# A graph layer ahead of three attention layers: block loop in four parts, one step of the open groups per part, row candidates taken one block later

## Chip, cores and metric

The kernel runs on one core of a Trainium2 chip. The metric is the device time of one launch in microseconds: the median of the timed runs is 3094.89 us (3094.21 to 3097.0, three runs). One further execution was recorded by the profiler; it took 2503.29 us.

## What is computed

The inputs are 3327 nodes with 256 features, `x`, and an adjacency matrix `adj` of 3327 x 3327 integers, 0 or 1, with about 16 ones in a row. Four layers follow one another. Cut to what matters here:

```
# layer 0
h = x @ Wt.T + bt                                  # 64 wide
s = leaky_relu(h @ Wa.T + ba, 0.2)                 # one number per row
w = softmax(where(adj > 0, s, -9e15), axis=1)
y = x + (w @ h) @ Wp.T + bp
x = gamma * (y - mean(y)) * rsqrt(var(y) + 1e-5) + beta
# layers 1, 2, 3
q, k, v = split(layer_norm(x) @ w_qkv)             # 8 heads of 32
attn = softmax(where(adj != 0, q @ k.T * scale, -inf))
x = x + (attn @ v) @ w_proj + b_proj
x = x + gelu(layer_norm(x) @ w1 + b1) @ w2 + b2
```

In layer 0 a row has one score for all its neighbours, so its softmax needs only the sum of `h` over the neighbours, the sum over all nodes and the number of neighbours.

## The kernel before

**Stages.** The rows form 26 blocks of 128. First `x` is loaded, `h` is computed and split into three bf16 parts beside a column of ones (`hs`). Then comes the block loop of layer 0 (L576 to L620), which reads the adjacency matrix once and makes two things of it: the neighbour sums and each row's list of neighbours. Then `order()` sorts the rows by their number of neighbours, and the three attention layers follow, which gather the keys and values of the listed neighbours one by one. Only the block loop and what runs in it is changed.

**One block.** `load(i)` brings 128 rows of `adj` (1.66 MB) into one of three int32 buffers by a DMA that SP issues; `cast(i)` turns them into bf16 on ACT (L269), into one of three buffers `abf`, whose pad columns POOL clears (L266). PE transposes the block in 26 pieces of 128 x 128, eight to a PSUM tile (L586; two such tiles, `pt`), and ACT copies each tile to `aT` by a sign function (L587). In the next iteration PE multiplies `aT` by `hs` in 26 matmuls (L590), and ACT copies the sum to `acc` (L600). For the lists DVE multiplies the block in place by the column numbers (L614, `num`) and takes the eight largest of each of 13 stretches of 256 columns (L617); these 104 candidates and the number of neighbours go to DRAM (L603, L604).

**Order in an iteration before.** The instructions are emitted in the order of the code and no scheduler moves them, so each engine works through its own queue in that order. Iteration `i` emits four times "eight transposes of block i, their sign copy, eight matmuls of block i-1" (the fourth time two of each); then the `acc` copy of block i-1 and its candidate DMAs; `cast(i+2)` and `load(i+4)`; one round of the open groups; the multiplication and the 13 maxima of block i; and a second round.

**Open groups and rounds.** When the last block of a group (`FIN`, mostly four blocks; the last groups have three, two and one) has its sums, `finish(f)` is opened for it. It is a generator: `steps(1)` is one round, in which each open group emits its next piece, up to its next `yield`. The pieces of a group of four, with the letters that the text uses:

- a (L404 to L437): counts and two score weights on DVE, their exponentials on ACT (L425, L426), prefix counts on PE, `seen` on POOL
- b (L439 to L453): the weighted neighbour sums `hn` on DVE
- c (L455 to L459): transposes of `hn` on PE, copy `nT` on ACT
- d (L461 to L471): product with `Wp` on PE (L466), addition to `x` on DVE (L470), addition of `bp` on POOL (L471)
- e (L473, L474): the rows' mean and variance on DVE (L126, L127), a power of -1/2 on POOL (L130)
- f (L476 to L484): one factor on DVE (L477), normalization on ACT (L479), gain and shift on POOL (L483, L484)
- g (L486): empty
- h (L487 to L489): the same moments for layer 1, and the rows to DRAM
- then for each of two pairs of blocks: i, normalization (DVE L137, then ACT L141); j, transposes on PE (L151) and their copy on ACT (L153); k and l, the q, k and v rows of one block each (PE L171 and L176, ACT L173 and L178) with their DMAs (L502, L503)

So a group of four has 16 pieces, and two rounds per iteration take it through eight iterations: in the steady part two groups are open at a time.

Of the kernel before, what the change touches and what calls it, by code (L numbers as in the profile page):

```python
# [8 lines left out]
FP = mybir.dt.float32  # L9
# [9 lines left out]
P = 128  # L19
# [12 lines left out]
NB = (N + P - 1) // P  # L32
# [28 lines left out]
def kernel(ctx: ExitStack, tc: tile.TileContext, ins, out: bass.AP):  # L61
# [136 lines left out]
    def node_list(b):  # L198

        t = nodes_[b]  # L200
        cd = t[:, 2 * D:2 * D + CAND]
        nr = (CAPS[b] + 7) // 8
        w = 8 * nr

        cg = lists.tile([P, CAND], FP, tag="cg", bufs=2, name=f"cg_{b}")
        nc.vector.scalar_tensor_tensor(cg, cd, 0.0, segb.rearrange("p s k -> p (s k)"), ALU.is_gt, ALU.mult)
        nc.vector.tensor_add(cg, cg, cd)
        ls = lists.tile([P, LW], FP, tag="ls", bufs=2, name=f"ls_{b}")
        for k in range(nr):
            nc.vector.max(out=ls[:, 8 * k:8 * k + 8], in_=cg)  # L210
            if k < nr - 1:
                nc.vector.match_replace(out=cg, in_to_replace=ls[:, 8 * k:8 * k + 8], in_values=cg, imm_value=0.0)
        em = lists.tile([P, LW], FP, tag="em", bufs=2, name=f"em_{b}")
        own = lists.tile([P, 1], FP, tag="own", bufs=2, name=f"own_{b}")
        nc.vector.tensor_scalar(em[:, :w], ls[:, :w], 0.5, None, ALU.is_lt)
        nc.vector.tensor_scalar(own, pf[:, b:b + 1], 1.0, None, ALU.add)
        nc.vector.scalar_tensor_tensor(ls[:, :w], em[:, :w], own, ls[:, :w], ALU.mult, ALU.add)
        nc.vector.tensor_scalar(idx[:, b, :w], ls[:, :w], -1.0, None, ALU.add)
        nc.vector.tensor_scalar(bias[:, b, :w], em[:, :w], NEG, None, ALU.mult)
        nc.vector.tensor_reduce(found[:, b, 0:1], em[:, :w], AX.X, ALU.add)  # L220
        nc.scalar.copy(found[:, b, 1:2], t[:, 2 * D + CAND:])


    with ExitStack() as st, tc.manual_schedule():
# [145 lines left out]
                h_rows(m - 1)  # L370
        cast(0)
        h_rows(len(PAIRS) - 1)
        cast(1)
        load(3)

        allb = [P, NB, H0]
        nc.vector.tensor_mul(rest, h_sb, wa_b[:, None, :].to_broadcast(allb))
# [14 lines left out]
        def finish(f):  # L392
# [62 lines left out]
            pt = big(f"ptn_{f}")  # L455
            for j in range(n):
                nc.tensor.transpose(pt[:H0, j * P:(j + 1) * P], hn[:, j, :], ident)
            nT = l0w.tile([H0, 4 * P], FP, tag="nT", bufs=1, name=f"nT_{f}")
            nc.scalar.copy(nT[:, :n * P], pt[:H0, :n * P])  # L459
            yield  # L460
            pps = []  # L461
            for j0 in range(0, n, 2):
                m = min(2, n - j0)
                ps = big(f"pp_{f}_{j0}").rearrange("p (b d) -> p b d", d=D)
                for j in range(j0, j0 + m):
                    nc.tensor.matmul(ps[:, j - j0, :], nT[:, j * P:(j + 1) * P], wpT, start=True, stop=True)  # L466
                pps.append((j0, m, ps))
            for j0, m, ps in pps:
                xi = x0[:, b0 + j0:b0 + j0 + m, :]
                nc.vector.tensor_add(xi, xi, ps[:, :m, :])  # L470
# [9 lines left out]
            for j0 in range(0, n, 2):  # L480
# [1 line left out]
                xi = x0[:, b0 + j0:b0 + j0 + m, :]  # L482
                nc.gpsimd.tensor_tensor(xi, xi, gam_b[:, None, :].to_broadcast([P, m, D]), ALU.mult)  # L483
                nc.gpsimd.tensor_add(xi, xi, bet_b[:, None, :].to_broadcast([P, m, D]))  # L484
            yield
            yield  # L486
            mv, rs = moments(views, f"q1_{f}")  # L487
            for i in blocks:
# [82 lines left out]
        def gains_in():  # L571
            pt = big("pt_cols")
            nc.tensor.transpose(pt[:, :P], cols, ident)
            nc.vector.tensor_copy(pv, pt[:, :48].rearrange("p (l k) -> p l k", l=3))

        for i in range(NB + 1):  # L576
            if i < NB:
                aTs[i] = l0w.tile([P, NB, P], BF, tag="aT", bufs=3, name=f"aT_{i}")
            if i:
                pa = ps_a.tile([P, 512], FP, tag="acc", name=f"pa_{i - 1}")  # L580
            for k0 in range(0, NB, 8):
                kn = min(8, NB - k0)
                if i < NB:
                    pt = ps_t.tile([P, 8, P], BF, tag="pt", name=f"pt_{i}_{k0}")
                    for m in range(kn):
                        nc.tensor.transpose(pt[:, m, :], abfs[i][:, (k0 + m) * P:(k0 + m + 1) * P], ident_bf)  # L586
                    nc.scalar.activation(aTs[i][:, k0:k0 + kn, :], pt[:, :kn, :], AF.Sign)  # L587
                if i:
                    for k in range(k0, k0 + kn):
                        nc.tensor.matmul(pa[:, :3 * H0 + 1], aTs[i - 1][:, k, :], hs[:, k, :],  # L590
                                         start=(k == 0), stop=(k == NB - 1))
            if i == 0:
                gains_in()
            if i == 1:
                bias_rows()
            if i:
                f, j = in_fin[i - 1]
                if j == 0:
                    accs[f] = l0w.tile([P, 4, 3 * H0 + 1], FP, tag="acc", name=f"acc_{f}")
                nc.scalar.copy(accs[f][:, j, :], pa[:, :3 * H0 + 1])  # L600
                cand = cands.pop(i - 1)
                nc.scalar.copy(cand[:, CAND:], accs[f][:, j, 3 * H0:])
                nc.sync.dma_start(cand_dr[(i - 1) * P:i * P, :], cand)  # L603
                nc.sync.dma_start(node_dr[(i - 1) * P:i * P, 2 * D:], cand)  # L604
            if i + 2 < NB:
                cast(i + 2)
                if i + 4 < NB:
                    load(i + 4)
            if i == NB:
                break  # L610
            steps(1)

            ab3 = abfs.pop(i).rearrange("p (s c) -> p s c", s=SEGS)
            nc.vector.tensor_mul(ab3, ab3, num)  # L614
            cands[i] = cand = l0w.tile([P, CAND + 1], FP, tag="cand", name=f"cand_{i}")
            for m in range(SEGS):
                nc.vector.max(out=cand[:, 8 * m:8 * m + 8], in_=ab3[:, m, :])  # L617
            if i and i - 1 in last_of:
                under.append(finish(last_of[i - 1]))
            steps(2 if i >= NB - 3 else 1)  # L620
        under.append(finish(last_of[NB - 1]))
        steps(1)
        under.append(order())
        while under:
# [465 lines left out]
```

## Time and profile before

| what | value |
|---|---|
| median of the timed runs | 3094.89 us |
| the profiled execution | 2503.29 us |
| its span, first to last instruction | 2501.5 us |
| its mean granted TensorE clock | 0.798 |
| busy in the span: PE, DVE, ACT, POOL | 1674.9, 1788.8, 794.1, 1485.3 us |
| start to the block loop | 0 to 42 us |
| block loop, to the last `acc` copy | 42 to 363.4 us |
| rest of layer 0 and of the sort, to the first gather of the layers | 363.4 to 414.3 us |
| attention layers | 414.3 to 2501.5 us |
| starts of the `acc` copies of blocks 0, 3, 7, 11, 15, 19, 25 | 51.8, 72.3, 110.8, 169.0, 223.7, 278.4, 363.4 us |

Times in the profile are microseconds from the span's start. In a view of waits a line names the instruction that waited, who ended the wait, then the total in us, the number of times and the longest. In a timeline a line has the start, the duration, the engine, the line of code, the operation with its output and inputs, and in brackets the idle time of the engine just before, with what ended it. In a table of windows each line has a stretch, its length, the busy time of PE, PE's weight loads, DVE, ACT and POOL with instruction counts, the granted clock, the share of the DMA engines and GB/s.

### The profile page before, as it was taken

What the parts mean: (1) busy time and instruction counts of PE and PEld (TensorE: products, weight loads), DVE (VectorE), ACT (ScalarE), POOL (GpSimd) and SP (SyncE); (2) the same over time, 40 slices, a digit from 0 to 9 for tenths busy, and PEclk for the clock granted to TensorE, in tenths of its full rate; (3) what the DMA queues carried; (4) which work ended last, traced back from release to release, by engine and by line L of the source; (5) the groups of instructions that cost most, each with busy time, mean ns of one, the idle gap of its engine ahead of it and who ended that gap; (6) DMA issues with size and microseconds to landing.
All of it is one profiled execution on the core that took longest, in us unless ns stands there. A gap on an engine that the chain in (4) does not pass through costs nothing. (4 is left out here: it accounts for less than half of the span.)

```text
span 2501.5 us, 25704 instructions
## 1 busy us (share of the span) xinstructions
PE 1674.9 (67%) x8346; PEld 1313.9 (53%) x8346; DVE 1788.8 (72%) x3214; ACT 794.1 (32%) x1464; POOL 1485.3 (59%) x1666
## 2 busy tenths in 40 slices
PE   7567663476678766683678787776837766766567
PEld 6445542355556545562566566554625655545455
DVE  6975684977789888743876787777437777777772
ACT  5766652132232222231143232222311323111222
POOL 1222235766667777615767677776157777777761
PEclk9788876588878887796778888878967888877777
DMA  6655515766567777616766677776167666666660
GB/s 238 210 169 167 158 60 173 210 197 176 165 188 215 209 211 208 182 49 212 205 186 200 189 213 217 212 210 187 46 198 207 194 200 192 201 204 190 198 181 11
DMA packets 158408, 452.79 MB, mean 181 GB/s; under 512 B 34367, under 2 KB 61641, under 8 KB 154937
## 3 DMA queue, kind: packets, MB, share of 16 engines
q0 software_dynamic: 111264, 363.68, 49.9%
q1 hardware_dynamic: 46636, 87.24, 10.6%
q8 instruction: 69, 1.13, 0.2%
q14 instruction: 75, 0.61, 0.1%
q10 hardware_dynamic: 364, 0.13, 0.0%
HBM read 410.64 MB, written 40.28 MB: 180 GB/s over the span
## 5 line engine op out<-in xcount | busy, mean ns | idle before, releaser
L758 POOL DMA_INDIRECT sl<-kv,idx x1290 | 1229.5, 953 | 400.1 <-issue 334.1
L805 PE MATMUL po<-ident,sl 128*128 128x128 f32 x2580 | 473.3, 347 | 601.5 <-DVE sl L802 600.7
L805 PEld LDWEIGHTS po<-ident,sl 128*128 128x128 f32 x2580 | 394.6, 180 | 673.6 <-DVE sl L802 665.1
L769 DVE TENSOR_TENSOR sl<-sl,qp 128x1024 f32<-128x1024 f32 (+1 forms) x354 | 397.1, 1122 | 239.5 <-DMA sl<-kv,idx 202.1
L770 DVE TENSOR_REDUCE sc<-sl 128x32 f32<-128x1024 f32 (+1 forms) x354 | 398.3, 1125 | 12.0
L802 DVE TENSOR_TENSOR sl<-sl,qp 128x1024 f32<-128x1024 f32 (+1 forms) x354 | 389.1, 1119 | 2.6
L685 PE MATMUL pu<-fT,w 128*128 128x256 f32 (+1 forms) x1344 | 329.3, 394 | 36.0 <-ACT fT L153 36.0
L698 PE MATMUL pd<-w,gT 128*128 128x256 f32 x1248 | 314.7, 407 | 28.4 <-ACT gT L689 28.4
L685 PEld LDWEIGHTS pu<-fT,w 128*128 128x128 f32 x1344 | 256.5, 207 | 77.4 <-ACT fT L153 44.7
L698 PEld LDWEIGHTS pd<-w,gT 128*128 128x128 f32 x1248 | 249.7, 206 | 76.1 <-ACT gT L689 32.6
L689 ACT ACTIVATE gT<-pu,pv 128x256 f32<-128x256 f32 (+1 forms) x336 | 134.9, 456 | 264.5 <-PE pu L685 260.4
L171 PE MATMUL pk<-wq,hT 128*128 128x512 f32 x312 | 177.9, 699 | 32.7 <-ACT hT L153 32.7
L141 ACT ACTIVATE xn_f<-x_sb,nmu_f,rsig_f 128x256 f32<-128x256 f32 x78 | 42.8, 593 | 366.3 <-DVE nmu_f L137 352.4
L703 DVE TENSOR_TENSOR x_sb<-x_sb,pd 128x512 f32<-128x512 f32 (+1 forms) x42 | 27.2, 648 | 166.0 <-PE pd L698 166.0
L811 ACT COPY oT<-po 128x256 f32<-128x256 f32 x78 | 29.0, 372 | 367.8 <-PE po L805 367.5
L666 DVE TENSOR_TENSOR x_sb<-x_sb,pp 128x512 f32<-128x512 f32 (+1 forms) x42 | 27.3, 649 | 133.3 <-PE pp L664 133.1
L617 DVE MAX8 cand<-abf 128x8 f32<-128x256 bf16 x338 | 113.0, 410 | 1.7
L171 PEld LDWEIGHTS pk<-wq,hT 128*128 128x128 f32 x312 | 63.2, 223 | 86.2 <-issue 40.6
L720 POOL DMA_INDIRECT kv<-kvr,perm x52 | 52.5, 1011 | 90.4 <-ACT kvr L173 76.9
L586 PE MATMUL pt<-ident_bf,abf 128*128 128x128 bf16 x676 | 59.9, 232 | 49.9 <-ACT aT L587 49.8
L664 PE MATMUL pp<-w_proj,oT 128*128 128x256 f32 x312 | 91.3, 441 | 1.1 <-issue 0.2
L176 PEld LDWEIGHTS pq<-wq,hT 128*128 128x128 f32 x312 | 64.3, 206 | 49.8 <-issue 39.3
(220 smaller groups left out, 2018.3 us busy)
## 6 DMA issues: line engine op xcount, KB each, us to landing
a<-in_adj_dram SPq DMA_DIRECT2D x25, 1663.5 KB
sl<-kv,idx POOLq DMA_INDIRECT x1290, 3.7
kv<-kvr SPq DMA_DIRECT2D x26, 256.0 KB
q<-qr SPq DMA_DIRECT2D x52, 128.0 KB
q<-q SPq DMA_DIRECT2D x52, 128.0 KB
w<-in_L_gnn_w_dram SPq DMA_DIRECT2D x6, 1024.0 KB
node<-x SPq DMA_DIRECT2D x26, 128.0 KB
node<-qr SPq DMA_DIRECT2D x26, 128.0 KB
```

What stands on the lines that cost most here:

```text
L171: nc.tensor.matmul(pk, hT[:, c, :], wq[:, c, D:], start=(c == 0), stop=(c == 1))
L176: nc.tensor.matmul(pq[:, :D], hT[:, c, :], wq[:, c, :D], start=(c == 0), stop=(c == 1))
L617: nc.vector.max(out=cand[:, 8 * m:8 * m + 8], in_=ab3[:, m, :])
L664: nc.tensor.matmul(pp[:, j, :], oT[:, c, j * P:(j + 1) * P], w["w_proj"][:, c, :], start=False, stop=(c == 1 and j == n - 1))
L685: nc.tensor.matmul(pu[:, a, :n * P], w["w1"][:, c, f * P:(f + 1) * P], fT[:, c, :n * P], start=(c == 0), stop=(c == 1))
L689: nc.scalar.activation(gT[:, f0 + a, :n * P], pu[:, a, :n * P], AF.Gelu_apprx_tanh, bias=pv[:, L - 1, 8 + f:9 + f])
L698: nc.tensor.matmul(pd[:, j, :], gT[:, f, j * P:(j + 1) * P], w["w2"][:, h * FH + f, :], start=False, stop=(h == 1 and f == FH - 1 and j == ...
L758: nc.gpsimd.indirect_dma_start(out=t[:, k - a, :], out_offset=None, in_=kv_dr[self.L][:, :], in_offset=bass.IndirectOffsetOnAxis(ap=idx[:, ...
L769: nc.vector.tensor_mul(kq, kq, self.qp[:, None, :D].to_broadcast([P, n, D]))
L770: nc.vector.tensor_reduce(self.sc[:, a:z, :], kq.rearrange("p s (h d) -> p s h d", h=HEADS), AX.X, ALU.add)
L802: nc.vector.tensor_mul(vv, vv, self.pw[:, a:z, :, None].to_broadcast([P, n, HEADS, HD]))
L805: nc.tensor.matmul(self.po[:, c, :], t[:, k, D + c * P:D + (c + 1) * P], ident, is_transpose=True, start=False, stop=(a + k == self.S - 1 ...
```

## The change

The iteration is cut into four parts, one for each PSUM tile of transposes. A part emits the transposes and the sign copy of block i; in the second part also `cast(i+1)` and `load(i+3)`; then the matmuls of block i-1; then a share of the candidate work of block i-1 instead of block i (the multiplication and 2 of the 13 maxima in the first part, then 4, 4 and 3); and one round of the open groups. The candidate work thus stands one block behind the transposes, and there are four rounds in each iteration instead of two, from the first iteration on; a new group opens at an iteration's end and has its first round in the next iteration. In `finish` piece c is cut in two (c1 the transposes, c2 the copy), d in two (d1 the product, d2 the additions), and the empty piece g is taken out: 17 pieces. `cast(0)` and `cast(1)` still stand ahead of the loop, `load(3)` now between them; a small tile of the list building, `own`, has one buffer instead of two.

```diff
@@ node_list
-        own = lists.tile([P, 1], FP, tag="own", bufs=2, name=f"own_{b}")
+        own = lists.tile([P, 1], FP, tag="own", bufs=1, name=f"own_{b}")
@@ ahead of the loop
+        load(3)
         cast(1)
-        load(3)
@@ finish
                 nc.tensor.transpose(pt[:H0, j * P:(j + 1) * P], hn[:, j, :], ident)
+            yield
             nT = l0w.tile([H0, 4 * P], FP, tag="nT", bufs=1, name=f"nT_{f}")
...
                 pps.append((j0, m, ps))
+            yield
             for j0, m, ps in pps:
                 xi = x0[:, b0 + j0:b0 + j0 + m, :]
                 nc.vector.tensor_add(xi, xi, ps[:, :m, :])
...
                 nc.gpsimd.tensor_add(xi, xi, bet_b[:, None, :].to_broadcast([P, m, D]))
-            yield
             yield
             mv, rs = moments(views, f"q1_{f}")
@@ the block loop
             if i:
                 pa = ps_a.tile([P, 512], FP, tag="acc", name=f"pa_{i - 1}")
-            for k0 in range(0, NB, 8):
+                ab3 = abfs.pop(i - 1).rearrange("p (s c) -> p s c", s=SEGS)
+                cand = l0w.tile([P, CAND + 1], FP, tag="cand", name=f"cand_{i - 1}")
+            for part, k0 in enumerate(range(0, NB, 8)):
...
                     nc.scalar.activation(aTs[i][:, k0:k0 + kn, :], pt[:, :kn, :], AF.Sign)
+                if part == 1:
+                    if 0 < i < NB - 1:
+                        cast(i + 1)
+                    if i + 3 < NB and i:
+                        load(i + 3)
+                    if i == 0:
+                        gains_in()
+                    if i == 1:
+                        bias_rows()
                 if i:
                     for k in range(k0, k0 + kn):
                         nc.tensor.matmul(pa[:, :3 * H0 + 1], aTs[i - 1][:, k, :], hs[:, k, :],
                                          start=(k == 0), stop=(k == NB - 1))
-            if i == 0:
-                gains_in()
-            if i == 1:
-                bias_rows()
+
+                    if part == 0:
+                        nc.vector.tensor_mul(ab3, ab3, num)
+                    for m in range(*((0, 2), (2, 6), (6, 10), (10, SEGS))[part]):
+                        nc.vector.max(out=cand[:, 8 * m:8 * m + 8], in_=ab3[:, m, :])
+                steps(1)
             if i:
...
                 nc.scalar.copy(accs[f][:, j, :], pa[:, :3 * H0 + 1])
-                cand = cands.pop(i - 1)
                 nc.scalar.copy(cand[:, CAND:], accs[f][:, j, 3 * H0:])
                 nc.sync.dma_start(cand_dr[(i - 1) * P:i * P, :], cand)
                 nc.sync.dma_start(node_dr[(i - 1) * P:i * P, 2 * D:], cand)
-            if i + 2 < NB:
-                cast(i + 2)
-                if i + 4 < NB:
-                    load(i + 4)
-            if i == NB:
-                break
-            steps(1)
-
-            ab3 = abfs.pop(i).rearrange("p (s c) -> p s c", s=SEGS)
-            nc.vector.tensor_mul(ab3, ab3, num)
-            cands[i] = cand = l0w.tile([P, CAND + 1], FP, tag="cand", name=f"cand_{i}")
-            for m in range(SEGS):
-                nc.vector.max(out=cand[:, 8 * m:8 * m + 8], in_=ab3[:, m, :])
-            if i and i - 1 in last_of:
-                under.append(finish(last_of[i - 1]))
-            steps(2 if i >= NB - 3 else 1)
-        under.append(finish(last_of[NB - 1]))
+                if i - 1 in last_of:
+                    under.append(finish(last_of[i - 1]))
         steps(1)
         under.append(order())
```

## The prediction

> **What bounds the kernel now.** I read the table of windows first, for the steady part: the four blocks from the `acc` copy at 169.0 to the one at 223.7 us, and the stretch after the loop.
>
> ```profile
> 169.00:223.70 54.70, 36.48 (x275) 27.85 (x274) 37.23 (x108) 36.42 (x52) 12.78 (x17) 0.81 0.53 172
> 363.40:414.30 50.90, 32.19 (x117) 17.61 (x116) 30.88 (x118) 17.22 (x42) 16.48 (x68) 0.83 0.35 111
> ```
>
> Four blocks take 54.7 us, PE, DVE and ACT are each busy for about 37, DMA for half. No engine is the bound: the loop is bound by waits among three in-order queues. The next four blocks (223.7 to 278.4) take the same 54.7. So I read the waits of the block loop (42 to 366 us), and then the timeline about the longest of them.
>
> ```profile
> PE pt L586 <- ACT aT L587: 49.8, 17, 7.2
> ACT xn_q L141 <- DVE nmu_q L137: 45.0, 10, 7.6
> DVE x L470 <- PE pp L466: 42.5, 10, 10.4
> ACT kvr L173 <- PE pk L171: 25.8, 11, 5.0
> ```
>
> ```profile
> 198.30 4.14 POOL L471 TENSOR_TENSOR x<-x,rowb 128x512 f32<-128x512 f32 x2 [10.61 <-DVE x L470]
> ...
> 201.41 4.35 DVE L617 MAX8 cand<-abf 128x8 f32<-128x256 bf16 x13
> 205.67 0.14 DVE L137 SCALAR_TENSOR_TENSOR nmu_q<-mv_q,rsig_q 128x2 f32<-128x2 f32 x1
> 205.85 1.09 ACT L141 ACTIVATE xn_q<-x,nmu_q,rsig_q 128x256 f32<-128x256 f32 x2 [7.59 <-DVE nmu_q L137]
> 207.90 1.01 PE L586 MATMUL pt<-ident_bf,abf 128*128 128x128 bf16 x8 [7.17 <-ACT aT L587]
> ```
>
> Piece i's 0.14 us factor stands on DVE behind the multiplication and 13 maxima; ACT waits 7.59 us for it with the next sign copies behind it, and so PE waits 7.17. That costs once per four blocks.
>
> ```profile
> 160.12 2.07 ACT L479 ACTIVATE x<-x,nm,rsig_l 128x256 f32<-128x256 f32 x4
> 161.35 1.27 POOL L483 TENSOR_TENSOR x<-x,rowb 128x512 f32<-128x512 f32 x1 [6.92 <-ACT x L479]
> ...
> 164.00 0.43 DVE L126 BATCH_NORM_STATS2 st_q<-x 128x6 f32<-128x256 f32 x1 [2.03 <-POOL x L484]
> ...
> 166.58 0.43 DVE L126 BATCH_NORM_STATS2 st_q<-x 128x6 f32<-128x256 f32 x1 [1.41 <-POOL abf L266]
> ```
>
> The chain e to h is visible here: ACT, four POOL operations of 1.27, then moments that DVE can begin only pair by pair. Even with the empty piece g between, DVE waits 2.03 and 1.41.
>
> **What the skill says.** (1) The Trainium skill, "TensorE: Matmul & The Clock Gate", section "Architectural detail": ACT and DVE are strict FIFO, only PE pulls weight loads forward. The 7.59 us wait agrees. (2) Same page, "What's actually happening": an idle PE drops to half clock and returns after sustained work. The trace agrees: after 7.17 idle, eight transposes take 1.01 instead of 0.61; a PE wait of 3.75 before 185.2 is followed by an L171 of 3.61 instead of 1.91. (3) "SBUF — State Buffer", section "Who interferes with whom": a DVE operation with two SBUF inputs contends with POOL's reads, one with a single input doesn't. Agrees: L614 takes 2.32 beside L471, 1.89 elsewhere.
>
> **The change, laid out by hand.** I put the four queues side by side with these durations: eight transposes and eight matmuls 1.13 from start to start; sign copy 0.9, the last 0.4; cast 2.96; `acc` and `cand` copies 0.5 together; multiplication 1.9, maxima 0.335 each, so DVE shares of 2.6, 1.4, 1.4 and 1.1. Pieces: a 3.2 on DVE, its exponentials ready 2.4 in; b 3.3; product of d 2.0 on PE, additions 1.4; e 2.2, then 1.3 to the power; f 2.07 on ACT, then POOL about 5.1; h ends 1.2 after POOL, the power 1.1 more; i 1.1, j 0.5 on PE and 1.0 on ACT; k or l 2.7 on PE at full clock (5.1 at half), copies 0.95. ACT's own work per block is 6.6 (the copies at 66.0 and 72.3 are 6.3 apart, without a group).
>
> A group now takes 17 rounds, so mostly one is open. The four iterations, ended by `acc` and `cand` copies, follow ACT:
> - A (l of the old group with a; b; c1; c2): ACT busy 8.9. It waits 1.6: for L171 and L176 in the first part and for the transposes behind them. 10.5 us.
> - B (d1; d2; e; f): busy 8.7. The second transposes stand behind the 2.0 us product: 1.4. The additions end 5 us into the iteration, POOL needs 2.6, the moments and the power follow; ACT reaches f with its four sign copies done and waits 2.8. 12.9 us.
> - C (h; i; j; k): busy 9.7. POOL ends gain and shift 3.5 into the iteration, the power comes 3 later, and ACT at i waits 1.9; then 2.1 for k's matmuls. 13.7 us.
> - D (l; i; j; k): busy 10.6, two waits of 1.4 and 2.1 for L171 and L176. 13.9 us.
>
> Sum 51.0 at full clock. PE now idles 4.7 and 5.0 in C and 3.4 in D; idles of that length are followed by half clock in the trace. Two of the four k/l then cost 2.4 more, two j 0.4 more: 56.6. I take 56, for 54.7 now.
>
> What goes: ACT's 9.4 for L137 and DVE's 10.2 for L466 (the two waits of the 54.7). The DVE wait costs nothing in itself: its cover is ACT's 37 busy us and its waits. What is late next is the chain d2 to i: its five rounds used to lie 6 us apart with a block of DVE work between them; now 2 to 3. Removing g brings h one round nearer to POOL's four operations.
>
> Moved beside other work, at nothing: the candidates one block behind take away L614's wait for transposes (2.2 per cycle, DVE only). L617 ends one iteration later; the candidate DMAs on SP wait for it and `load` stands behind them, but it is issued two iterations, over 12 us, ahead of its cast, as before, and DMA is busy for 0.53. If that cover fails, a load's 7 us (1.66 MB at 240 GB/s) comes on the path. `load(3)` still waits for `cast(0)`. L266 stands on POOL behind h's power; the instruction order of the changed program lists the cast of iteration C as waiting for its DMA alone, so only the next block's last transposes need L266. The wait on `own` is among DVE's own operations. `finish`'s DMAs keep their order among themselves; k's rows are issued once per part rather than twice in a row.
>
> Block by block: to the copy at 72.3 no group is open, ACT bounds at 6.3 per block: 0. Blocks 4 to 7: before 38.5, since the first group gets two rounds per iteration and is alone; now a whole cycle without l, A 12.8 as its DVE lead is missing, 53.3 plus 1 to 5 for clock: +18. Blocks 8 to 11: before 58.2, now 56: -2. Blocks 12 to 19: 2 x 1.5 = +3. Blocks 20 to 25: before 85.0; now 10.5 + 12.9 + 13.7, then 16 (D with a to c of the group of three), 15, and 14 for the last without sign or cast, 82.1, plus 5.6: +3. After the loop: before 7, 10 and 11 pieces are left of the last three groups, now 4, 9 and 12. The last takes 44 us from 365.5 for its 11, 4 each: +4 for one more, -4 for fewer companions (-6 to +5): 0. Sum +22; with full clock throughout +15 - 7 - 7 - 3 = -2. I take +15, nearer the throttled end.
>
> On the profiled execution: 2503.3 + 15 = 2518. The timed median is 591.6 us above it; the profile doesn't show where, so I carry the difference over unchanged: 3094.9 + 15 = 3110. If it scaled with the time it would be +19, inside the range.
>
> **Rivals.**
> - Faster: the chain e to i is hidden. Place: ACT at f and i. The waits of 2.8 and 1.9 vanish if the parts of B and C last 3.9 us or more on the other engines, and if the closer spacing keeps PE at full clock. The cycle is 51.0 - 4.7 = 46.3: four later cycles give 4 x -8.4 = -34, the first +10: -24, 3071; if k/l are covered too, another 4 x 3.5 less: 3057. For it: ACT is busy only 37 of 54.7. Against: each piece still needs the one before from another engine, one short part earlier.
> - No change: full clock, chain as laid out: -2, 3093.
> - Worse: POOL contention (L471 took 4.14 for two, where I took 2.6) and half clock in all four k/l instead of two. Place: iterations B, C and D; it decides once the multiplication of the next part meets L471, or PE idles over 3.4 us in A too. 1.5 + 4.8 = 6.3 per cycle, over the four later cycles +25 on top of the +15: 3135; half of it, 3122. For it: both have been seen in this trace. Against: L471 now stands beside maxima, which read one operand.
> - The change doesn't do what it says: would the rounds be taken unevenly, two groups would stay open. The code forbids it: one call per part.
>
> **Chances.** Forecast, with its own range 3102 to 3120, 0.41; worse 0.14; no change 0.12; faster 0.33. Within 0.2% means 3088.7 to 3101.1, about what a measurement of this kernel can tell from no change. Faster 0.33, same 0.12, slower 0.55. The range reaches from the faster rival's second figure to the worse one's end: 3057 to 3135.
>
> **What would show it.** Right: cycles of four blocks of 54 to 58 us between `acc` copies; no wait of ACT for L137 above 3; new waits of ACT for L477 and of DVE for L484; L171 of 3.6 in iteration C. The step for the first group is right if block 7's copy comes at about 128 instead of 110.8. It is wrong if ACT's waits for L477 and L137 together are under 2 us per four blocks, or if the cycle is under 50. The layers' part should keep its 2087 us.

## The result, and the profile after

| | before | after |
|---|---|---|
| median of 12 timed runs each | 3094.55 us (3086.81 to 3104.66) | 3092.6 us (3075.4 to 3098.8) |
| ratio, 95% interval | | 0.9984 (0.9966 to 1.0003) |
| profiled execution | 2503.29 us | 3086.38 us |
| starts of the `acc` copies 3, 7, 11, 15, 19, 25 | 72.3, 110.8, 169.0, 223.7, 278.4, 363.4 | 74.8, 127.6, 178.7, 229.9, 281.1, 365.1 |
| first gather of the layers (L187) | 414.3 us | 412.4 us |

The change made no difference that these runs can tell: -2 us, where +15 was forecast. The attention layers of every kernel here take some 590 us more in most sets of runs than in one (the kernel before has a median of 2503.6 us in one set below and 3091 to 3115 in the rest), so ratios are formed within a set only, and what the change does is read from the stage ahead of the layers, which repeats within 5 us (first gather at 414.3 and 418.9 before, 412.4 and 411.0 after).

The lines of the changed kernel shift: transposes L586 are now L591, sign copy L592, matmuls L604, multiplication L608, maxima L610, `acc` copy L616; L466, L470, L471 are L467, L472, L473; L477, L479 are L479, L481; L483, L484 are L485, L486.

The table of windows of the changed kernel, for a steady cycle of four blocks and for the stretch from the last `acc` copy to the first gather (columns as before):

```profile
178.70:229.90 51.20, 35.91 (x278) 26.62 (x276) 36.51 (x107) 35.97 (x53) 11.48 (x16) 0.83 0.56 183
365.06:412.40 47.34, 26.39 (x86) 13.58 (x84) 29.90 (x106) 12.44 (x32) 15.54 (x68) 0.71 0.28 90
```

The busy times are those of before (36, 37, 36); the cycle went from 54.7 to 51.2, so 3.5 us of waiting went. The cycles from block 8 to block 19 all take 51.1 or 51.2. Which waits are left, from the view of waits in that cycle:

```profile
DVE abf L608 <- PE pt L591: 8.4, 1, 8.4
PE pn_q L151 <- ACT xn_q L141: 8.2, 2, 5.5
ACT kvr L173 <- PE pk L171: 7.2, 4, 2.7
...
PE pt L591 <- ACT aT L592: 4.9, 3, 2.8
...
DVE st_q L126 <- POOL x L486: 3.1, 2, 1.7
ACT xn_q L141 <- DVE nmu_q L137: 2.4, 1, 2.4
ACT x L481 <- DVE nm L479: 2.2, 1, 2.2
```

The two long waits of before (ACT for L137 in one piece of 7.6, DVE for L466 of 10.1) are gone. In their place stand many waits of 1.5 to 8 us, most of them of an engine for the one group's next link. (The 8.4 of L608 is another kind: DVE has run out of candidates and of the group's work in iteration D, and stands ahead of the next multiplication until the block's last transposes are made.) The timeline of iteration C shows a stretch of that chain:

```profile
201.99 1.27 POOL L486 TENSOR_TENSOR x<-x,rowb 128x512 f32<-128x512 f32 x1
203.29 0.43 DVE L126 BATCH_NORM_STATS2 st_q<-x 128x6 f32<-128x256 f32 x1 [1.67 <-POOL x L486]
...
205.87 0.43 DVE L126 BATCH_NORM_STATS2 st_q<-x 128x6 f32<-128x256 f32 x1 [1.40 <-POOL x L486]
...
207.32 1.02 POOL L130 TENSOR_TENSOR rsig_q<-rsig_q,mhalf 128x4 f32<-128x4 f32 x1 [1.49 <-DVE rsig_q L129]
...
208.64 1.09 ACT L141 ACTIVATE xn_q<-x,nmu_q,rsig_q 128x256 f32<-128x256 f32 x2 [2.44 <-DVE nmu_q L137]
209.30 1.18 PE L151 MATMUL pn_q<-ident,xn_q 128*128 128x128 f32 x4 [5.52 <-ACT xn_q L141]
...
211.15 3.38 PE L171 MATMUL pk<-wq,hT 128*128 128x512 f32 x4
...
214.36 1.03 PE L176 MATMUL pq<-wq,hT 128*128 128x256 f32 x4
214.56 0.59 ACT L173 COPY kvr<-pk 128x512 f32<-128x512 f32 x1 [2.73 <-PE pk L171]
```

POOL, DVE, POOL, ACT, PE, ACT: from 202.0 to 214.6 each line with a bracket starts when the one named there ends. PE waits 5.52 and its next products take 3.38 in place of 1.91. It is not the only stretch of slow rows in a cycle; these are the rows of d's product and of iteration D:

```profile
189.12 1.99 PE L467 MATMUL pp<-wpT,nT 64*128 64x256 f32 x8
...
224.03 1.18 PE L151 MATMUL pn_q<-ident,xn_q 128*128 128x128 f32 x4 [2.65 <-ACT xn_q L141]
...
225.89 2.83 PE L171 MATMUL pk<-wq,hT 128*128 128x512 f32 x4
```

As to the layers, their table of windows before and after (the first is of the kernel before):

```profile
420.00:2501.50 2081.50, 1401.44 (x6323) 1101.87 (x6323) 1492.70 (x2340) 546.25 (x1106) 1379.60 (x1460) 0.79 0.63 184
```

```profile
420.00:3084.50 2664.50, 1525.93 (x6323) 1167.23 (x6323) 1487.57 (x2340) 542.34 (x1105) 1381.37 (x1458) 0.72 0.49 144
```

Instruction counts agree to 2, and the busy times of DVE, ACT and POOL to 5 us; PE is busy 125 us longer. Most of the 583 us are waits. The longest of a new kind have no releaser in this program (the profile calls it "remote"), in the waits of the changed kernel's layers:

```profile
ACT gT L689 <- remote: 328.3, 20, 27.4
...
ACT oT L811 <- remote: 204.5, 9, 41.6
```

Since the timed runs of both kernels hold it, it is no part of the change.

### The profile page after: what moved, and what is told of

Same layout as the page of the kernel before. It is cut to its first block, busy times and chain, and to the rows that moved or that the text cites. A ratio compares the mean times of both kernels' runs of the same rounds, so it can differ in the third digit from the quotient of the medians.

```text
span 3084.5 us, 25707 instructions
## 1 busy us (share of the span) xinstructions
PE 1806.9 (59%) x8346; PEld 1380.3 (45%) x8346; DVE 1775.9 (58%) x3214; ACT 790.0 (26%) x1464; POOL 1479.2 (48%) x1666
## 4 chain that ended last, share of the span: by engine, by line
PE 25%; another core or an unknown queue 19%; issue 16%; DVE 13%; POOL 7%; ACT 5%; DMA 2%; SPq 0%; DVEq 0%; POOLq 0%; ACTq 0%
PE pd L698 7%; POOL sl L758 6%; PE po L805 5%; PE pu L685 4%; PE pk L171 4%; DVE sl L769 3%; DVE sl L802 3%; PE pp L664 2%; DVE sc L770 2%; PE pq L176 2%; DMA sl<-kv,idx 1%; ACT gT L689 1%; DMA q<-q 1%; ACT L689 1%
## 5 line engine op out<-in xcount | busy, mean ns | idle before, releaser
L805 PE MATMUL po<-ident,sl 128*128 128x128 f32 x2580 | 493.6, 354 | 690.0 <-DVE sl L802 521.4
L805 PEld LDWEIGHTS po<-ident,sl 128*128 128x128 f32 x2580 | 410.0, 185 | 764.6 <-DVE sl L802 558.2
L698 PE MATMUL pd<-w,gT 128*128 128x256 f32 x1248 | 355.8, 445 | 224.5 <-ACT gT L689 194.5
L685 PE MATMUL pu<-fT,w 128*128 128x256 f32 (+1 forms) x1344 | 356.7, 411 | 99.0 <-issue 50.7
L698 PEld LDWEIGHTS pd<-w,gT 128*128 128x128 f32 x1248 | 274.6, 227 | 293.3 <-ACT gT L689 208.1
L685 PEld LDWEIGHTS pu<-fT,w 128*128 128x128 f32 x1344 | 267.7, 216 | 151.7 <-issue 61.7
L689 ACT ACTIVATE gT<-pu,pv 128x256 f32<-128x256 f32 (+1 forms) x336 | 134.9, 458 | 542.9 <-remote 328.3
L171 PE MATMUL pk<-wq,hT 128*128 128x512 f32 x312 | 199.8, 775 | 89.2 <-ACT hT L153 78.0
L130 POOL TENSOR_TENSOR rsig_f<-rsig_f,mhalf 128x2 f32<-128x2 f32 (+1 forms) x42 | 29.2, 696 | 292.3 <-DVE rsig_f L129 273.7
L720 POOL DMA_INDIRECT kv<-kvr,perm x52 | 52.6, 1012 | 225.0 <-ACT kvr L173 161.0
L811 ACT COPY oT<-po 128x256 f32<-128x256 f32 x78 | 29.1, 374 | 475.0 <-remote 204.5
L171 PEld LDWEIGHTS pk<-wq,hT 128*128 128x128 f32 x312 | 70.6, 248 | 155.5 <-ACT hT L153 88.8
L610 DVE MAX8 cand<-abf 128x8 f32<-128x256 bf16 x338 | 116.5, 411 | 1.9
L130 POOL TENSOR_TENSOR rsig_h<-rsig_h,mhalf 128x2 f32<-128x2 f32 (+1 forms) x28 | 19.5, 695 | 196.2 <-DVE rsig_h L129 196.2
```

Of the source, the lines that this page charges most:

```text
L171: nc.tensor.matmul(pk, hT[:, c, :], wq[:, c, D:], start=(c == 0), stop=(c == 1))
L685: nc.tensor.matmul(pu[:, a, :n * P], w["w1"][:, c, f * P:(f + 1) * P], fT[:, c, :n * P], start=(c == 0), stop=(c == 1))
L689: nc.scalar.activation(gT[:, f0 + a, :n * P], pu[:, a, :n * P], AF.Gelu_apprx_tanh, bias=pv[:, L - 1, 8 + f:9 + f])
L698: nc.tensor.matmul(pd[:, j, :], gT[:, f, j * P:(j + 1) * P], w["w2"][:, h * FH + f, :], start=False, stop=(h == 1 and f == FH - 1 and j == ...
L805: nc.tensor.matmul(self.po[:, c, :], t[:, k, D + c * P:D + (c + 1) * P], ident, is_transpose=True, start=False, stop=(a + k == self.S - 1 ...
```

## The experiments

The edits of e7 and e11 are shown against the kernel before, that of e8 against e2, that of e10 against e4, all others against the changed kernel. Theory 1: the cycle is the latency of the chain of pieces of the one open group. Theory 2: PE's idle times and the half clock after them are the cost. Theory 3: what counts is the place of the candidates. "Cycle" is half the time between the `acc` copies of blocks 11 and 19, two cycles of four blocks. "Loop" is the time from the `acc` copy of block 3 to the first gather, which leaves out how early the first loads came (the copy of block 3 lies between 68 and 75 us in all profiles). Ratios are to the kernel before in the same set.

| kernel | steps per block, groups open | candidates | blocks 4-7 | cycle | loop | ratio (95%) |
|---|---|---|---|---|---|---|
| before | 2, two | own block | 38.5 | 54.7 | 342.0 | 1 |
| before, again | 2, two | own block | 41.4 | 54.6 | 344.0 | |
| after | 4, one | behind, spread | 52.8 | 51.2 | 337.6 | 0.9984 (0.9966 to 1.0003) |
| after, again | 4, one | behind, spread | 52.0 | 51.2 | 336.9 | 0.9984 (0.997 to 0.9997) |
| e1 copies a step later | 4, one | behind, spread | 48.9 | 54.6 | 349.5 | 1.0031 (1.0015 to 1.0046) |
| e2 two steps | 2, two | behind, spread | 35.8 | 43.5 | 305.6 | 0.9855 (0.9835 to 0.9876) |
| e3 PE kept busy | 4, one | behind, spread | 50.8 | 49.8 | 333.7 | 0.997 (0.9955 to 0.9984) |
| e4 own block | 4, one | own block | 60.2 | 61.6 | 387.6 | 1.0216 (1.0188 to 1.0244) |
| e7 behind alone | 2 at the end, two | behind, one stretch | 36.4 | 52.3 | 336.9 | 0.9982 (0.9969 to 0.9994) |
| e8 one stretch | 2, two | behind, one stretch | 38.2 | 48.0 | 326.4 | 0.9949 (0.992 to 0.9978) |
| e9 alternate | 4 stops, two | behind, spread | 36.2 | 43.1 | 309.9 | 0.9886 (0.9857 to 0.9915) |
| e10 parts only | 2, two | own block | 41.5 | 46.1 | 320.1 | 0.9905 (0.9874 to 0.9935) |
| e11 one step moved | 2, two | own block | 41.1 | 47.7 | 315.8 | 0.9906 (0.9881 to 0.9932) |
| e12 steps in pairs | 4, one | behind, spread | 51.5 | 52.8 | 340.8 | 0.9975 (0.9961 to 0.9988) |
| e13 groups drained | all at once | behind, spread | 73.9 | 73.2 | 485.2 | 1.0508 (1.0473 to 1.0542) |

**The kernel before again.**

> The kernel before, run once more, because its profiled execution lasted 2503 us where all its timed runs lasted about 3095. Every theory expects the stage before the layers to be the same as in the profile shown (first gather of a layer, L187, at 414 us, within 1 us). If the 590 us were a property of that one execution, this profile has a layers' part of about 2665 us, like that of the changed kernel.

Its first gather came at 418.9, 4.5 us later and not within the 1 us expected; 2.5 of that is there at the copy of block 3 already, so the loop repeats within 2 us. The layers' part did not turn out 2665: 2090.8 us from the first gather, in a set in which all 20 timed runs of the kernel before lay between 2499 and 2512. So 2503 is not the accident of one execution: it is a level that holds for a whole set of runs.

**e1, copies of k and l a step later.**

```diff
-                    kv, q = qkv_rows(l0w, big, wq1, hT[...], 1, f"1_{i}")
+                    pk, pq = qkv_products(big, wq1, hT[...], f"1_{i}")
+                    yield
+                    kv = ...; nc.scalar.copy(kv, pk)
+                    q = ...; nc.scalar.copy(q, pq[:, :D])
                     ... DMAs ...
-                    yield
```

> The changed kernel with the copies of k and l (L174, L178) and their DMAs put one round behind the products that they read, nothing else. Theory 1 (the loop waits for the chain of the one open group, piece by piece, above all ACT): the waits of ACT for L171 and L176, 8.6 us of a cycle of 51.2, go; the cycle of four blocks falls to 44 to 47 us, the first gather of the layers from 412.4 to about 390, the time by 15 to 25 us. Theory 2 (PE's idle time and half clock are the cost): the copies are not the cost, PE still idles ahead of j, the cycle stays at 49 to 51. Theory 3 (the place of the candidates is what counts): no change, 51.

A miss for every theory: 54.6. From its table of windows and its waits:

```profile
176.20:230.90 54.70, 40.18 (x275) 29.34 (x274) 36.86 (x108) 35.26 (x53) 11.25 (x16) 0.78 0.51 171
```

```profile
ACT aT L606 <- PE pt L605: 17.1, 5, 4.9
```

ACT no longer waits for L171, but ahead of the sign copies (L606 here), 17.1 us in place of 2.0. Four of these five waits are for transposes that stand on PE behind the same products, which lasted up to 3.78 us; the longest, 4.9, is for transposes behind d's product, which took 3.77 here in place of 1.99. So most of the 8.6 us were not ACT's to save: PE is in the chain at that place. How much of the 3.4 us per cycle that this kernel is slower by comes from the lower clock (0.78 for 0.83) was not separated.

**e2, two steps per block.**

```diff
-                steps(1)
+                if part % 2 or i >= NB - 3:
+                    steps(1)
```

> The changed kernel with a step of the open groups only in the second and the fourth part: two rounds per block instead of four, so that two groups are open as before the change; candidates a block behind, the four parts and the split pieces are kept. Theory 1: each piece has half a block's work between it and the next, the waits on ACT shrink, a cycle of 46 to 49 us instead of 51.2; the first group's cost of 14 us goes (block 7 at about 114 instead of 127.6); after the loop 3 us more. Sum -20 us or more on the first gather. Theory 2: PE's idles are fewer too, about 49. Theory 3 (candidates alone): the cycle stays at 51 and only the first group's cost goes, -14.

```profile
152.70:196.70 44.00, 35.23 (x275) 27.16 (x272) 37.35 (x107) 35.48 (x52) 11.27 (x17) 0.84 0.64 214
```

Cycles of 44.0 and 43.0, better than theory 1 expected; theories 2 (49) and 3 (51) miss. Blocks 4 to 7 take 35.8. Same instructions, the same busy times within 1 us, the same granted clock as after (0.84 and 0.83): so it isn't the clock. The loop is shorter than that of both others (305.6 us for 342.0 and 337.6), and the time is 0.9855 of before.

**e4, candidates in their own block, four steps.**

```diff
-                    if part == 0:
-                        nc.vector.tensor_mul(ab3, ab3, num)
-                    for m in range(...):  nc.vector.max(...)
-                steps(1)
+                if part < 3:
+                    steps(1)
...
+            if i < NB:
+                ... multiplication and 13 maxima of block i ...
+            steps(1)
```

> The changed kernel with the candidates put back to where they were: multiplication and 13 maxima of block i together at the end of iteration i, the fourth step of the groups behind them; four steps per block kept. Theory 1 (the chain): pieces on DVE in the first part now stand behind 6.4 us of candidates, and DVE's multiplication waits for the transposes; the cycle is 54 to 58 us, 10 to 20 us on the first gather over the changed kernel. Theory 3 (the candidates' place is what gained the 3.5 us per cycle): the cycle is back at 54.7 or above, as in the kernel before. Theory 2: no change, 51.

61.6: theory 1's direction, above its range, and theory 3's too, so it doesn't divide them; theory 2, which expected 51, falls. From the waits of its cycle (the multiplication is L617 here, the transposes L589):

```profile
DVE abf L617 <- PE pt L589: 30.6, 4, 10.1
...
ACT xn_q L141 <- DVE nmu_q L137: 8.4, 2, 6.2
```

DVE waits up to 10.1 us for the block's transposes before it begins its 6.4 us of candidates, and ACT's next link stands behind these. With four steps the lag and the spread together are worth 10.4 us per cycle.

**After again, e7, e8, e3** share one set of timed runs.

> The changed kernel again, beside the others on the same chip. Every theory expects the block loop of its profile shown (cycles of four blocks of 51.2 us, first group ended at about 127 us), and a time 2 us below the kernel before, within 6.

As expected: 51.2, block 7 at 126.1, a median of 3089.7 for 3094.7.

e7 is the kernel before with the lag alone, and with the cast and the load at the place that the lag needs:

```diff
-            steps(1)
-            ... multiplication and 13 maxima of block i ...
+            steps(1)
+            if i:
+                ... multiplication and 13 maxima of block i - 1 ...
```

> The kernel before with one part of the change alone: the multiplication and the 13 maxima are those of the block before (i-1 in place of i), in one stretch at their old place; the cast stands where the change puts it, since it needs the buffer that the candidates read. Groups as before: two steps a block, unsplit pieces, the empty piece. Lag theory (what gains is that DVE no longer waits for the block's last transposes ahead of 6.4 us of candidates): a cycle of 44 to 47 us in place of 54.6, the time 30 to 40 us under the kernel before. Split theory (what gains is that a piece on DVE stands behind at most 2.6 us of candidates in place of 6.4): 53 to 55, within 8 us of the kernel before. Theory 1 of the record, the chain of the groups alone: 54 to 55.

52.3, -2.4: under the split theory's 53 and far from the lag theory's 44 to 47, which falls for this order of steps. DVE's wait for the transposes goes, but the wait that counts is still there, behind the same 6.4 us of candidates (waits from 164.05 to 215.52):

```profile
ACT xn_q L141 <- DVE nmu_q L137: 9.7, 2, 7.8
```

e8 is e2 with all candidates in the fourth part:

```diff
-                    if part == 0:
+                    if part == 3:
                         nc.vector.tensor_mul(ab3, ab3, num)
-                    for m in range(*((0, 2), (2, 6), (6, 10), (10, SEGS))[part]):
+                    for m in range(*((0, 0), (0, 0), (0, 0), (0, SEGS))[part]):
```

> The two-round kernel (changed kernel with steps only in the second and fourth part, cycle 43 to 44 us), with the multiplication and all 13 maxima of block i-1 in one stretch in the fourth part instead of spread over four. Lag theory: the cycle stays within 2 us of 44, the time within 8 us of 2470. Split theory: the piece in the fourth part stands behind 6.4 us of DVE, the cycle goes back to 50 to 54, the time by 30 us or more.

48.0: between the two, so spreading is worth 4.5 us of e2's gain and not the 6 to 10 of the split theory.

e3 keeps PE from idling ahead of j:

```diff
+        for _ in range(fill):                       # 18 or 8
+            nc.tensor.matmul(pf_, ident_bf, rhs, start=True, stop=True)
         ... the transposes of xn into the same tile ...
```

> The changed kernel with 18 (first pair) or 8 (second pair) bf16 matmuls of no use ahead of j's transposes, in the same PSUM tile, which the transposes then overwrite, so that PE doesn't stand idle while it waits for ACT's L141. Theory 2 (the half clock after such idles costs): L171 in iteration C falls from 3.4 to about 1.9 us and the cycle from 51.2 to 47.5 to 49. Theory 1: PE is off the path while ACT is at i; the cycle stays within 1 us of 51.2, or grows if the matmuls come in the way of the transposes of the next part.

```profile
174.40:223.50 49.10, 41.15 (x303) 29.42 (x301) 36.60 (x107) 35.79 (x52) 11.25 (x16) 0.90 0.57 191
```

```profile
185.38 3.78 PE L470 MATMUL pp<-wpT,nT 64*128 64x256 f32 x8
...
205.17 0.93 PE L154 MATMUL pn_q<-ident,xn_q 128*128 128x128 f32 x4 [1.40 <-ACT xn_q L141]
...
207.02 1.98 PE L174 MATMUL pk<-wq,hT 128*128 128x512 f32 x4 [0.64 <-ACT hT L156]
```

In this cycle both slow L171 (here L174), in C and D, are cured: 1.98 in place of 3.38 and 2.83. The clock rises from 0.83 to 0.90, and the cycle lasts 49.1, 2.1 less. Between the `acc` copies, C takes 13.1 us for 14.7 and D 13.4 for 14.2, together 2.4 less; B takes 0.4 more, since the half clock came at d's product instead (L470 here, 3.78 for 1.99). In the cycles before and after it only the L171 of D is cured (the one in C still takes 3.25 and 3.55), and they last 50.7 and 50.5. The rows that e3 cures were longer by 1.5 + 0.9 for L171 and twice 0.25 for L151 (1.18, here 0.93), 2.9 in all. So the half clock at these two places costs about 2.4 of 51.2, and theory 2 explains a small part. Theory 1 allowed 1 us and misses the mean of 49.8 by 0.4. A slow stretch in B of the changed kernel, where eight matmuls of L604 take 1.50 and then 1.39 for 0.85, is not priced by any run. The kernel before pays the same kind of price: two of its four L171 take 3.61 and 3.78 in a cycle.

**e9 and e10** share another. e9 keeps four stops per block, but each advances one group only:

```diff
-                steps(1)
+                for f, e in list(opened.items()):
+                    if (f % 2 == part % 2 or i >= NB - 3) and next(e, 0) == 0:
+                        del opened[f]
```

> The changed kernel with four steps per block kept, but each step advances one group only: groups of even number in the first and third part, of odd number in the second and fourth (in the last three blocks all of them in every part). So two groups are open, and the pieces of one group stand two parts apart. Distance theory (four rounds cost because consecutive pieces of one group stand only one part apart, so that each finds its input not ready): a cycle of 41 to 45 us, first gather at about 375 to 380 us, 32 to 40 us under the changed kernel. Number theory (it is the number of stops among transposes and products that costs, since each puts a piece between PE's and ACT's work): the cycle stays at 49 to 52, like the changed kernel.

Cycles of 46.8 and 39.3, mean 43.1: the distance theory holds, the number theory falls. The second of these cycles:

```profile
193.24:232.56 39.32, 32.71 (x290) 25.06 (x288) 36.42 (x106) 35.29 (x52) 11.42 (x16) 1.00 0.75 249
```

It comes within 3 us of DVE's busy time, and PE has its full clock without any filler. The loop's end is worse than e2's (blocks 20 to 25 take 97.9 for 90.7), so the loop as a whole is 4 us longer.

e10 completes the square with two steps and the candidates in their own block:

```diff
-                if part < 3:
+                if part == 1 or (part < 3 and i >= NB - 3):
                     steps(1)
```

> The kernel with the candidates in block i's own iteration, in one stretch at its end as before the change, four parts and split pieces as in the changed kernel, but two steps per block: one in the second part and one behind the candidates. It fills the square of number of steps and place of candidates (two and own block: this one; four and own block: 61.6 us per cycle measured; two and a block behind: 43.5; four and a block behind: 51.2). If the two effects add, 61.6 - 7.7 = 54 us, within 1.5, and the time equals that of the kernel before within 8 us. If the step placed between the parts is a gain by itself (distance between the pieces), 48 to 51. Number theory: below 56 in any case.

46.1, not 54: the two effects don't add. Against it, four steps in the same order cost 15.5 (e4), and the lag with the spread is worth 2.6 with two steps but 10.4 with four.

**e11 and e12.** e11 is the kernel before with its first step moved:

```diff
+                if k0 == 8 and i < NB:
+                    steps(1)
...
-            steps(1)
-
             ab3 = abfs.pop(i).rearrange("p (s c) -> p s c", s=SEGS)
```

> The kernel before with one edit: its first step of a block, which stood behind the acc copy and the cast, is made behind the second of the four parts. Unsplit pieces, the empty piece, the candidates in their own block and the cast stay as they were. Distance theory (half a block's transposes and products between consecutive pieces of a group is what gains): a cycle of 45 to 49 us in place of 54.6, as with two steps in the other kernel of that order (46.1), the time 18 to 30 us under the kernel before. If the split of the pieces, the missing empty piece or the cast's place gained those 8.5 us: 53 to 55, within 8 us of the kernel before.

47.7. The one edit is worth 7.0 of e10's 8.6 us; the split pieces, the missing empty piece and the cast's place bring 1.6 at most. Its waits in the cycle, where the kernel before, profiled again, has 9.4, 10.1 and 7.2 in the same three places:

```profile
ACT xn_q L141 <- DVE nmu_q L137: 6.5, 2, 3.9
...
DVE x L470 <- PE pp L466: 3.0, 2, 2.9
...
PE pt L586 <- ACT aT L587: 0.2, 1, 0.2
```

e12 takes the four steps of the changed kernel two at a time:

```diff
-                steps(1)
+                steps(2 * (part % 2))
```

> The changed kernel with its four steps of a block taken two at a time, in the second and the fourth part, one group open as in the changed kernel. Distance theory: two consecutive pieces of the one group stand side by side with nothing between them, the waits grow, a cycle of 54 to 62 us in place of 51.2, first gather 12 to 40 us later. Number theory (stops among transposes and products cost): half as many stops, 44 to 48. If only the number of pieces per block counts, 51.

52.8: the number theory falls again, but so does the distance theory as put: side by side, the pieces cost only 1.6 more than a part apart. What e2, e9 and e12 leave is neither the stops nor the space between two pieces, but that one group alone must go through all its pieces in four blocks.

**e13, a group drained in one go,** asks for that chain's length.

```diff
-                steps(1)
...
-                    under.append(finish(last_of[i - 1]))
+                    for _ in finish(last_of[i - 1]):
+                        pass
```

> The changed kernel with no steps in the parts: each group is taken through all its pieces in one go where it is opened, at the end of the iteration of its last block. So three blocks of four run bare and the fourth shows a group's chain with nothing of the next blocks between its pieces. Bare blocks: 6.6 us apart (as blocks 1 to 3 of the changed kernel), 26.5 for four. If the chain alone takes 42 to 51 us (latency theory: the changed kernel's cycle of 51.2 is the length of one chain, the blocks hide beside it), the cycle is 69 to 77. If it takes about 25 (sum theory: in the changed kernel almost nothing of the chain lies beside the blocks), the cycle is about 51, no longer than the changed kernel's. In between: part of each.

```profile
74.37 0.17 DVE L405 TENSOR_SCALAR dc<-acc 128x4 f32<-128x4 f32 x1 [2.25 <-ACT acc L615]
...
82.59 3.77 PE L467 MATMUL pp<-wpT,nT 64*128 64x256 f32 x8 [0.67 <-ACT nT L460]
...
119.99 0.37 ACT L178 COPY qr<-pq 128x256 f32<-128x256 f32 x1 [0.28 <-PE pq L176]
```

```profile
74.00:126.47 52.47, 25.69 (x120) 15.84 (x120) 21.52 (x70) 17.49 (x31) 11.13 (x14) 0.67 0.24 81
126.47:147.86 21.39, 14.64 (x156) 13.93 (x156) 15.63 (x38) 19.47 (x22) 0.20 (x2) 0.84 0.77 261
```

The lines are the chain's first and last and its slow product of d: from 74.4 to 120.4, 46 us. The first window has one block and a whole group, the second three bare blocks (7.1 each on average). The five such openings take 52.5, 51.4, 52.6, 51.6 and 51.0, mean 51.8; less a bare block of 6.6 the chain of a group of four lasts 45 us with almost no other work in its way. The cycle is 73.2, inside the latency theory's 69 to 77; the sum theory's 51 falls.

So most of the changed kernel's 51.2 is the length of one chain, once per cycle. That the other 6 us are block work in its way is not shown, since the drained chain ran at a lower granted clock (0.67): by its rows d's product, j, k and l and c's transposes took 3.3 us more there than in the changed kernel's cycle, so that the chain is nearer 42 at the clock of the changed kernel (an estimate from the rows of both traces). Two groups at half the pace have two cycles for a chain, which is then no bound, and 39 to 47 are left, for engines that are busy for 33 to 41.

## Why the prediction was wrong, by its own steps

- **What bounds the kernel (waits, no engine): right**, with the word too general. The steady waits are of two kinds: a bad place in DVE's queue (before), and the latency of one chain (after).
- **ACT's 9.4 for L137 and DVE's 10.2 for L466 go, the chain d2 to i is late next: right**, with the waits named in advance: ACT for L479 (then L477) 2.2 for 2.8, ACT for L137 2.4 for 1.9, DVE for L486 3.1. No wait for L137 over 3: right.
- **A 10.5, B 12.9, C 13.7, D 13.9 at full clock: right in sum by luck**: 9.7, 12.5, 14.7, 14.2 in the cycle from 178.7, sum 51.2 for 51.0. But the clock was not full (0.83): A and B were priced 1.2 too high, and C and D, where the slow L171 lie, took 1.3 more than priced. With both L171 cured, e3 has 13.1 and 13.4 for C and D, so these were priced high too.
- **The step that failed: "Two of the four k/l then cost 2.4 more, two j 0.4 more: 56.6. I take 56."** The two slow L171 are there, in C and in D, but they lasted 1.5 and 0.9 us longer, not 2.4 each with L176 (which stayed at 1.03); j took 1.18 twice, 0.6 more than the 0.60 at 180.9 in the kernel before. C and D with both L171 cured are 2.4 shorter (e3). So the term for half clock was 5.6 and should have been about 2.4. That is 3.2 of the 5.4 us from 56.6 to 51.2; the other 2.2 are iterations priced generously (0.8, 0.4, 0.6 and 0.5). So the cycle is 51.2 for 56, and blocks 8 to 25 gave -7.1, -3.6, -3.4 and -1.1, together -15.2, where the forecast had -2, +3 for two cycles and +3: 19 of the 24 us between the block-by-block sum of +22 and the -2 of the traces. (The +3 for two cycles is 2 x 1.3 by the forecast's own 56 and 54.7.)
- **The rule behind that step, half clock after idleness: right.** That an idle PE comes back at half clock (the Trainium skill, "TensorE: Matmul & The Clock Gate", section "What's actually happening") is seen behind the waits of 5.52 and 2.65. The page has both changes of the clock at about 3.4 us, of idleness or of sustained work; here 2.65 were enough in D, and in e3's cycle the rows stay slow from 184.0 to 193.6 us with PE at work without a gap, so the measurements decide.
- **First group +18: right in kind, +14.3** (+10.6 between the two second profiles). Block 7 came at 127.6 where 128 was forecast, but that is in part luck: the loop began 2.5 later, and the blocks took 3.7 less than forecast. e2, e9 and e10, with two steps, give 35.8 to 41.5 for these blocks, so the loss is that of the four steps.
- **Blocks 0 to 3 and the stretch after the loop at 0:** +2.5 and -3.5. The first is the spread of the loads' start (the kernel before again has its copy of block 3 at 74.9); that the twelfth piece would cost 4 and fewer companions save 4 was off by 3.5.
- **Candidates a block behind "at nothing": nearly right for the order of the kernel before, wrong for the new one.** DVE's wait of 2.2 for the transposes, which was to go, became 8.4 (L608), at a time when DVE has no other work. e7 finds 2.4 per cycle in the old order; e4 finds that the four steps would cost 10.4 per cycle more without it and its spread. The layout by hand had the lag in it, so the sum is not wrong by it, but the prediction's account of what carries the gain is.
- **"The sum is +22; with full clock -2. I take +15."** The rival without change had 3093 from full clock and an unchanged chain, and came out at 3092.6. It had the cycle (51.0) and the first group (+15) right, but not for its reason: the clock was 0.83, and the durations laid out too long made up for it. The worse rival's contention is not seen: the two operations of L473 take 2.50 beside the maxima, where L471 took 4.14 in the kernel before. (The section on SBUF that the prediction cites frees single-input operations from contention only outside their two-port modes; of these operations the runs show the maxima.) Of the faster rival, ACT's waits at f and i stayed (2.2 and 2.4). No case saw the larger fact: the change has a gain of 11 us per cycle in it (e2: a step between the parts, candidates behind and spread), and gives 7.7 of it back, and 17 for the first group (52.8 for 35.8), by taking four steps instead of two. The 2518 for the profiled execution and the 2087 for the layers can't be judged, since the profile after has the longer layers.

In the path from one kernel to the other by the runs: a step moved between the parts, 54.7 to 46.1 (e10, 7.0 of the 8.6 by the move alone); four steps, one group, 46.1 to 61.6 (e4); candidates behind and spread, 61.6 to 51.2. Or over e2: to 43.5, and 7.7 back for the four steps. What stays open is why the layers have two levels; and how the 45 us of the chain divide among its links was not measured.

## What to carry to other kernels

- Before a chain of dependent pieces is taken faster, compare its length alone with the time it is given: a chain of 42 to 45 us in a cycle whose engines are busy for 37 is the bound; two chains at half the pace leave it covered. A drained run, all pieces in one go, measures the length.
- Look first for the one step that stands in a bad place of a queue: one `steps(1)` moved ahead of 6.4 us of DVE work was worth 7 us of 54.7 per cycle, twice what the whole change brought (3.5).
- Price a half clock from its rows one by one and test it with work of no use that keeps PE going, and look where the half clock goes then: 2.9 us of longer matmuls were worth 2.4 us per cycle, where 5.6 had been charged, and 0.4 came back at another product.

## What was not expected of the hardware

Two levels of one kernel's time, 20 runs at 2503.6 us (2499.4 to 2511.6) in one set and 54 at 3094.7 (3077.4 to 3106.8) in another, were not expected; both sets carry the same chip number, 12. The lines above show ACT standing 328 us ahead of L689 and 205 ahead of L811 with no releaser in the program, and a DMA share of 0.49 for 0.63. The granted clock of the layers is lower too, 0.72 for 0.79, but PE is busy only 125 us longer in 583.

All ten profiles of the longer level (after, after again, e3 and e7 to e13) have such "remote" waits in their layers, and none of the five of the shorter (before, before again, e1, e2, e4) has one. No kernel was profiled on both levels. But none of the ten has a "remote" wait ahead of the first gather, and in each set the difference of the timed medians from the kernel before is that of the loops to within 9 us (e13, the slowest: 14). So the loops can be compared across the levels. No run here shows the cause of the levels.
